# Corner sums through a PSUM tile, and a share of the corner multiply on GpSimd, in a deformable-convolution stage

## The chip, the cores and the metric

The kernel runs on one core of a Trainium2 chip. The metric is device time in microseconds for one execution, in fp32 throughout. The names of the engines in the profile are PE (TensorE), DVE (VectorE), ACT (ScalarE), POOL (GpSimd) and SP (the queue of SyncE, which only issues transfers). PEld is TensorE's loading of weights.

## The reference

The whole computation is a two-layer block on x of shape 2 x 128 x 64 x 64: a deformable convolution with four branches, a mixture of experts over tokens, a selective scan, and a second mixture of experts. The change lies in the first of these. For each output position and each tap of a branch, a learned offset gives a fractional position, and the input is sampled there bilinearly from four corners:

```
wy = (py - y0)[:, None]
wx = (px - x0)[:, None]
v00 = gather(y0, x0);      v01 = gather(y0, x0 + 1)
v10 = gather(y0 + 1, x0);  v11 = gather(y0 + 1, x0 + 1)
return v00 * (1 - wy) * (1 - wx) + v01 * (1 - wy) * wx + v10 * wy * (1 - wx) + v11 * wy * wx
...
sampled = bilinear_sample(x, py, px) * mask[:, None]
return jnp.einsum('bckhw,ock->bohw', sampled, reg_w.reshape(O, C, k * k))
```

The kernels of the four branches are 1x1, 1x1, 3x3 and 7x7, so that there are 1 + 1 + 9 + 49 = 60 taps (NTAP) for each position. C is 128, and each branch has 256 output channels.

## The kernel before

Positions are handled in groups of 512: four tiles (GT = 4) of 128 positions, one position to a partition. Each of the two images has 8 groups, so that there are 2 x 8 x 60 = 960 steps, called taps below. For every image a table in device memory holds, for each position, the 4 x 128 values of its four corners side by side, so that one row of 2 KB serves one sample.

The method `sample` runs the 60 taps of one group. For a tap it uses a buffer `v` of shape 128 x 4 x 512 (four tiles, and in each the four corners of 128 channels); there are six such buffers. `gather` (line 705) fills it with four indirect transfers, one for each tile, that are issued by GpSimd with row numbers from the tile `idx`. Then, on VectorE:

- line 746 multiplies all 2048 elements of a partition with the corner weights `pw`, broadcast over the 128 channels. `pw` is a copy in PSUM of the weights `w4`, made on line 738 for 30 taps at a time;
- line 748 adds corners 2 and 3 onto corners 0 and 1 (1024 elements);
- line 749 adds corner 1 onto corner 0 (512 elements).

All of these work in place in `v`. TensorE then transposes the four tiles into the PSUM tile `pst` (line 111), which is what frees `v`; ScalarE copies `pst` to `st` (line 753); and two taps later `product` multiplies `st` by the tap's weights `regw` on TensorE (line 773) and accumulates over the taps of a branch.

The order of work on TensorE, VectorE, ScalarE, GpSimd and SP is the order in which the program is written. The gathers of tap t+1 are written ahead of the arithmetic of tap t, and GpSimd, which has only gathers in this stage, runs ahead of VectorE as far as the six buffers go. At the end of each tap, pieces of other work are put in: `conv.step()`, the offset convolution (line 402 on TensorE) and the corner indices and weights of groups to come (lines 499 to 587, mostly VectorE), and `rest.step()`, the normalization of the second image, and, while the second image is sampled, the rest of the layers for the first one. After the sampling, in the last 2157 us, come the scan (lines 1420 to 1481) and the second mixture of experts.

PSUM has eight banks. While the first image is sampled `pw` takes one, `pst` two, `out` two, and the offset convolution with its companion two; while the second is sampled the last two go to the other work.

Of the kernel before, what the change touches and what calls it, by code (L numbers as in the profile page):

```python
# [10 lines left out]
F32 = mybir.dt.float32  # L11
I32 = mybir.dt.int32
AF = mybir.ActivationFunctionType
ALU = mybir.AluOpType
AX = mybir.AxisListType
PSUM = bass.MemoryType.PSUM
# [3 lines left out]
P = 128  # L20
B = 2
C = 128
# [3 lines left out]
GT = 4  # L26
# [9 lines left out]
NO = 3 * NTAP  # L36
TW = H + 3
E0 = 8
E1 = 64
HID = 512  # L40
DS = 16
# [143 lines left out]
class L0Conv:  # L185
# [416 lines left out]
    def run(self, build, after):  # L602

        env, tc, nc = self.env, self.env.tc, self.env.nc
        pools = lambda ctx: lambda name, bufs, **kw: ctx.enter_context(tc.tile_pool(name=name, bufs=bufs, **kw))
        with ExitStack() as ctx:
            pool = pools(ctx)
            self.rp, self.regw = pool("l0rw", 1), {}
            self.ip = pool("l0i", 2)
            self.vp = pool("l0v", 6)  # L610
            self.stp = pool("l0s", 2)
            self.pending, self.held = [], deque()
            first = ctx.enter_context(ExitStack())
            self.open_offsets(pools(first))
            for i in range(2):
                nc.vector.memset(self.padc[i], 0.0)
            psum = ctx.enter_context(ExitStack())
            right = lambda name: pools(psum)(name, 1, space=PSUM, side="right")
            self.p_f = deque([right("l0po")])
            cur = self.new_group(self.ip)  # L620
            with (
                tc.tile_pool(name="nrm", bufs=3) as sp,
                tc.tile_pool(name="nrmp", bufs=4, space=PSUM) as pp,
            ):
                xs = []
                for g in range(NG):
                    if g % GT == 0:
                        x = self.vp.tile([P, GT, 4 * C], F32, name="v")
                    xs.append(x[:, g % GT, :])
                    nc.sync.dma_start(out=xs[g], in_=env.d["x"][0, :, g * 512 : (g + 1) * 512])  # L630
                xn = self.vp.tile([P, GT, 4 * C], F32, name="v")
                self.load_weights()
                for _ in self.zero_table(0):
                    pass
                own = lambda g: xn[:, g % GT, :].rearrange("p (j c) -> p j c", c=C)
                norms = [self.norm_group(0, g, sp, pp, "nrm", x, own(g)) for g, x in enumerate(xs)]
                together(norms[:2], 2)

                stage = self.rows(0, 0)
                self.sum_weights()  # L640
                others = Side()
                others.add(mixed(norms[2:], 3))
                for _ in range(24):
                    others.step()
                offsets = self.offset_stream([(0, 0, cur)], stage)
                while others.todo:
                    next(offsets)
                    for _ in range(3):
                        others.step()
                self.load_chunk(0)  # L650
                for _ in self.norm_end(0):
                    pass
                for _ in offsets:
                    pass
            self.p_w = pool("l0pw", 1, space=PSUM)
            self.p_t = pool("l0pt", 2, space=PSUM)
            self.p_o = pool("l0py", 2, space=PSUM)
            self.pending = [(n, functools.partial(self.load_chunk, c)) for n, c in ((1, 1), (3, 2))]
            early = psum.enter_context(ExitStack())
            p_m = pools(early)("l0pm", 1, space=PSUM, side="right")  # L660

            def more():

                early.close()
                self.p_f.append(right("l0po2"))
                yield


            conv, rest = Side(), Side()
            self.late, self.made = deque(), [0, 0]  # L670
            rest.add(self.norm(1, p_m, "misc"), more(), build)
            ahead = {}

            def runs():
                for g in range(1, NG):
                    ahead[g] = self.new_group(self.ip)
                    yield 0, g, ahead[g]
                    yield 1, g - 1, None
                yield 1, NG - 1, None

            conv.add(self.offset_stream(runs()))
            for g in range(NG):
                self.sample(0, g, *cur, conv, rest, 2 if g else 3, lambda: ahead.get(g + 1))
                cur = ahead.get(g + 1)
            conv.drain()
            rest.drain()
            psum.close()
            first.close()
            side = ctx.enter_context(tc.tile_pool(name="l0ps", bufs=2, space=PSUM))
            rest.add(after(0, side))  # L690
            cur = self.load_group(1, 0)
            for g in range(NG):
                nxt = self.load_group(1, g + 1) if g + 1 < NG else None
                self.sample(1, g, *cur, conv, rest, 2, lambda: nxt)
                cur = nxt
            for f in self.late:
                f()
            for _, f in self.pending:
                f()
            self.pending = []  # L700
            rest.drain()
# [10 lines left out]
    def sample(self, b, g, idx, w4, conv, rest, pace, after):  # L712

        env, nc = self.env, self.env.nc
        pw, vs = None, {}
        new = lambda: self.vp.tile([P, GT, 4 * C], F32, name="v")

        def fetch(idx, t):
            if t in vs:
                v = vs.pop(t)  # L720
                self.gather(b, v, idx, t, range(2, GT))
            else:
                v = new()
                self.gather(b, v, idx, t, range(GT))
            return v

        if b == 0 and g == 0:
            for i in range(6):
                vs[i] = new()
                self.gather(b, vs[i], idx, i, range(0, 2))  # L730
        if not self.held:
            self.held.append(fetch(idx, 0))
        for br, (k, _) in enumerate(BRANCH):
            for t in range(FIRST[br], FIRST[br] + k * k):
                tw = t % HT
                if tw == 0:
                    pw = self.p_w.tile([P, GT, HT, 4], F32, name="pw")
                    nc.vector.tensor_copy(pw, w4[:, :, t : t + HT, :])
                if t + 1 < NTAP:
                    self.held.append(fetch(idx, t + 1))  # L740
                elif after():
                    self.held.append(fetch(after()[0], 0))
                v = self.held.popleft()
                v4 = v.rearrange("p j (q c) -> p j q c", q=4)
                w = pw[:, :, tw, :].unsqueeze(3).to_broadcast([P, GT, 4, C])
                nc.vector.tensor_tensor(v4, v4, w, ALU.mult)  # L746
                up = v4[:, :, 0:2, :]
                nc.vector.tensor_tensor(up, up, v4[:, :, 2:4, :], ALU.add)  # L748
                nc.vector.tensor_tensor(v4[:, :, 0, :], v4[:, :, 0, :], v4[:, :, 1, :], ALU.add)  # L749
                pt = self.p_t.tile([P, GT, P], F32, name="pst")  # L750
                transpose4(nc, env.ident, pt, [v4[:, j, 0, :] for j in range(GT)])
                st = self.stp.tile([P, 512], F32, name="st", bufs=3)
                nc.scalar.copy(st, pt.rearrange("p j t -> p (j t)"))  # L753
                self.late.append(functools.partial(self.product, b, g, br, t, st))
                if len(self.late) > 2:
                    self.late.popleft()()
                due = [f for n, f in self.pending if n == 0]
                self.pending = [(n - 1, f) for n, f in self.pending if n]
                for f in due:
                    f()  # L760
                conv.step()
                for _ in range(pace):
                    rest.step()
# [128 lines left out]
class L0Ffn:  # L892
# [3 lines left out]
    def __init__(self, env, dp, wp, gp):  # L896

        nc, d = env.nc, env.d
        self.env, self.dp, self.gp = env, dp, gp
        self.rw = wp.tile([P, E0], F32, name="rw")  # L900
        self.rb = wp.tile([P, E0], F32, name="rb")
        self.ew = wp.tile([P, E0 * C], F32, name="ew")
        self.eb = wp.tile([E0, C], F32, name="eb")
        self.tri = wp.tile([P, E0, E0], F32, name="tri")
        nc.sync.dma_start(out=self.rw, in_=d["router_w"])
# [993 lines left out]
```

## Time and profile before

| | |
|---|---|
| median of 3 runs | 7887.33 us (7886.47 to 7905.6) |
| the profiled execution's own time | 7901.31 us |
| its span, first to last instruction | 7898.7 us |
| sampling stage | to about 5742 us of the span |
| busy: PE, DVE, ACT, POOL | 68%, 77%, 25%, 64% of the span |
| mean granted clock of TensorE | 0.806 |

The profile has one line for each group of instructions: line, engine, operation, output and inputs, shapes, count; then the group's busy time in us and the mean of one in ns; then the idle time of the engine just ahead of these instructions, and what ended most of it. In a list of waits, a row says who waited for whom, the us in total, how many times and the longest. "issue" means that nothing the profile shows was waited for. In a timeline, a row has its start, its duration, and in brackets the idle time before it.

### The profile page before, as it was taken

To read this page: it belongs to the slowest core of one execution; us is meant where nothing else is said; L and a number is where in the kernel's file an instruction comes from. 1 tells how busy PE (TensorE), PEld (TensorE's weight loads), DVE (VectorE), ACT (ScalarE), POOL (GpSimd) and SP (SyncE) were. 2 spreads that over 40 slices of the span, in tenths; PEclk is the share of its full clock that TensorE was granted. 3 is DMA by queue.
4 is the path that set the end of the run, shared out by engine and by line. 5 is a ranking of instruction groups with operands and counts; after the bars stand their busy time and mean duration, and the time that the engine had idled before them with its cause. 6 is when DMAs were issued, how large, how long until landed. Compare 5 with 4: busy or idle time off the path is not lost. (4 is left out here: it accounts for less than half of the span.)

```text
span 7898.7 us, 67414 instructions
## 1 busy us (share of the span) xinstructions
PE 5390.6 (68%) x21313; PEld 3209.2 (41%) x21313; DVE 6077.1 (77%) x6780; ACT 1992.0 (25%) x3838; POOL 5031.9 (64%) x4589
## 2 busy tenths in 40 slices
PE   4667777667776757656666878865565679756668
PEld 3344444444444424324334555532233456412124
DVE  5878878888887887788898667787756665789992
ACT  1211111111111113211111222211163255455540
POOL 4777777777777777777777666676743334357640
PEclk8888788888788878878878778877886788877789
DMA  7887767777676778877777777777754344434444
GB/s 223 261 267 214 224 207 223 214 219 219 210 221 208 224 228 270 265 255 234 240 237 217 217 218 218 228 224 222 206 172 141 107 114 113 114 131 146 146 137 149
DMA packets 645198, 1596.67 MB, mean 202 GB/s; under 512 B 168020, under 2 KB 253180, under 8 KB 640876
## 3 DMA queue, kind: packets, MB, share of 16 engines
q0 software_dynamic: 307200, 1006.88, 42.5%
q1 hardware_dynamic: 306156, 537.52, 21.4%
q10 hardware_dynamic: 31488, 47.97, 1.7%
q8 instruction: 171, 2.80, 0.1%
q14 instruction: 183, 1.50, 0.1%
HBM read 1478.65 MB, written 115.83 MB: 202 GB/s over the span
## 5 line engine op out<-in xcount | busy, mean ns | idle before, releaser
L705 POOL DMA_INDIRECT v<-table,idx x3840 | 4070.0, 1060 | 1628.2 <-issue 1033.8
L746 DVE TENSOR_TENSOR v<-v,pw 128x2048 f32<-128x2048 f32 x960 | 2192.0, 2283 | 665.7 <-DMA v<-table,idx 466.9
L773 PE MATMUL out<-st,regw 128*128 128x512 f32 x3840 | 2270.7, 719 | 187.6 <-issue 118.6
L753 ACT COPY st<-pst 128x512 f32<-128x512 f32 x960 | 557.7, 585 | 4227.9 <-remote 1887.3
L111 PE MATMUL pst<-ident,v 128*128 128x128 f32 x3840 | 730.7, 318 | 1133.6 <-issue 962.4
L748 DVE TENSOR_TENSOR v<-v 128x1024 f32<-128x1024 f32 x960 | 1177.2, 1226 | 34.6 <-remote 1.6
L1420 POOL TENSOR_TENSOR db<-du,bcb 128x512 f32<-128x512 f32 x512 | 656.8, 1288 | 845.3 <-DVE da L1471 698.8
L773 PEld LDWEIGHTS out<-st,regw 128*128 128x128 f32 x3840 | 807.2, 233 | 864.6 <-issue 779.9
L111 PEld LDWEIGHTS pst<-ident,v 128*128 128x128 f32 x3840 | 522.4, 164 | 1512.3 <-issue 1284.6
L1443 PE MATMUL py<-sc,ident 128*128 128x512 f32 x1024 | 660.7, 752 | 230.7 <-DVE sc L1481 230.3
L1471 DVE TENSOR_TENSOR_SCAN da<-da,state,db 128x512 f32<-128x512 f32 x512 | 657.1, 1283 | 183.2 <-ACT da L1427 137.6
L749 DVE TENSOR_TENSOR v<-v 128x512 f32<-128x512 f32 x960 | 664.4, 692 | 33.0
L402 PE MATMUL po<-wa,win 128*128 128x147 f32 x2112 | 381.7, 303 | 118.1 <-issue 110.8
L402 PEld LDWEIGHTS po<-wa,win 128*128 128x128 f32 x2112 | 334.3, 201 | 228.7 <-issue 228.6
L1443 PEld LDWEIGHTS py<-sc,ident 128*128 128x128 f32 x1024 | 200.4, 229 | 529.9 <-DVE sc L1481 438.0
L1146 PEld LDWEIGHTS ps<-ipw,hs 128*120 128x120 f32 x2816 | 356.0, 207 | 121.7 <-ACT X L1108 56.4
L1146 PE MATMUL ps<-ipw,hs 128*120 128x64 f32 x2816 | 355.1, 290 | 55.2 <-ACT X L1108 40.5
L1481 DVE TENSOR_TENSOR sc<-da,bcb 128x512 f32<-128x512 f32 x512 | 354.2, 692 | 43.0 <-PE py L1443 0.5
L1427 ACT ACTIVATE da<-delta,w_A_log 128x512 f32<-128x512 f32 x512 | 354.0, 692 | 18.7 <-DVE delta L1383 2.8
L1154 PE MATMUL ps<-tm,X 120*88 120x48 f32 x2048 | 216.1, 280 | 52.1 <-ACT Y L1108 35.5
L1154 PEld LDWEIGHTS ps<-tm,X 120*88 120x88 f32 x2048 | 211.0, 187 | 98.7 <-ACT Y L1108 47.4
L402 PEld LDWEIGHTS po<-wb,win 128*128 128x128 f32 x960 | 164.2, 210 | 117.2 <-issue 117.1
(296 smaller groups left out, 4704.3 us busy)
## 6 DMA issues: line engine op xcount, KB each, us to landing
bcb<-bc SPq DMA_DIRECT2D x256, 512.0 KB
regw<-in_regw SPq DMA_DIRECT2D x192, 640.0 KB
v<-table,idx POOLq DMA_INDIRECT x3840
yd<-ys ACTq DMA_DIRECT2D x128, 256.0 KB
yc<-yd SPq DMA_DIRECT2D x32, 1024.0 KB
gb<-gd SPq DMA_DIRECT2D x16, 2048.0 KB
wt<-in_weight SPq DMA_DIRECT2D x32, 1024.0 KB
tm<-pos SPq DMA_DIRECT2D x16, 1440.0 KB
```

Of the source, the lines that this page charges most:

```text
L111: nc.tensor.transpose(ps[:, j, :], s, ident)
L402: m()
L705: self.env.nc.gpsimd.indirect_dma_start(out=v[:, j, :], out_offset=None, in_=self.table[b], in_offset=bass.IndirectOffsetOnAxis(ap=idx[:, ...
L746: nc.vector.tensor_tensor(v4, v4, w, ALU.mult)
L748: nc.vector.tensor_tensor(up, up, v4[:, :, 2:4, :], ALU.add)
L749: nc.vector.tensor_tensor(v4[:, :, 0, :], v4[:, :, 0, :], v4[:, :, 1, :], ALU.add)
L753: nc.scalar.copy(st, pt.rearrange("p j t -> p (j t)"))
L773: nc.tensor.matmul(self.out[half], self.regw[t // CH][:, t % CH, half * P : (half + 1) * P], st, start=first, stop=last,)
L1146: nc.tensor.matmul(ps[:, k, :], patch, own, start=True, stop=True)
L1420: nc.gpsimd.tensor_tensor(dbs[u], pieces[k]["du"][:, half, :], bcb[u // 2][:, 0, :], ALU.mult)
L1443: nc.tensor.matmul(py[k, half], by, what, start=first, stop=last)
L1471: nc.vector.tensor_tensor_scan(s, s, dbs.pop(u), state[:, half, n : n + 1], ALU.mult, ALU.add)
```

## The change

In every second tap (t odd, EVERY = 2) GpSimd multiplies the fourth corner with its weight, which it reads from `w4` in SBUF, and VectorE multiplies only the other three. In all taps the four corners are summed by three additions of 512 elements instead of one of 1024 and one of 512; the partial sum lies in a new PSUM tile `low`, of one bank, and the last addition writes corner 0 of `v`.

```
+EVERY = 2
...
+            self.p_r = pool("l0pr", 1, space=PSUM)
...
-                w = pw[:, :, tw, :].unsqueeze(3).to_broadcast([P, GT, 4, C])
-                nc.vector.tensor_tensor(v4, v4, w, ALU.mult)
-                up = v4[:, :, 0:2, :]
-                nc.vector.tensor_tensor(up, up, v4[:, :, 2:4, :], ALU.add)
-                nc.vector.tensor_tensor(v4[:, :, 0, :], v4[:, :, 0, :], v4[:, :, 1, :], ALU.add)
+                side = t % EVERY == EVERY - 1
+                if side:
+                    w = w4[:, :, t, 3:4].to_broadcast([P, GT, C])
+                    nc.gpsimd.tensor_tensor(v4[:, :, 3, :], v4[:, :, 3, :], w, ALU.mult)
+                end = 3 if side else 4
+                w = pw[:, :, tw, 0:end].unsqueeze(3).to_broadcast([P, GT, end, C])
+                nc.vector.tensor_tensor(v4[:, :, 0:end, :], v4[:, :, 0:end, :], w, ALU.mult)
+                low = self.p_r.tile([P, GT, C], F32, name="low")
+                nc.vector.tensor_tensor(low, v4[:, :, 0, :], v4[:, :, 1, :], ALU.add)
+                nc.vector.tensor_tensor(low, low, v4[:, :, 2, :], ALU.add)
+                nc.vector.tensor_tensor(v4[:, :, 0, :], low, v4[:, :, 3, :], ALU.add)
```

## The prediction

> **What bounds the kernel now.** I read the page first, then busy time by stretch, the waits of GpSimd and VectorE, and two timelines of the same ten microseconds. The page gives the per-tap prices.
>
> ```profile
> L705 POOL DMA_INDIRECT v<-table,idx x3840 | 4070.0, 1060 | 1628.2 <-issue 1033.8
> L746 DVE TENSOR_TENSOR v<-v,pw 128x2048 f32<-128x2048 f32 x960 | 2192.0, 2283 | 665.7 <-DMA v<-table,idx 466.9
> L748 DVE TENSOR_TENSOR v<-v 128x1024 f32<-128x1024 f32 x960 | 1177.2, 1226 | 34.6 <-remote 1.6
> L1420 POOL TENSOR_TENSOR db<-du,bcb 128x512 f32<-128x512 f32 x512 | 656.8, 1288 | 845.3 <-DVE da L1471 698.8
> L749 DVE TENSOR_TENSOR v<-v 128x512 f32<-128x512 f32 x960 | 664.4, 692 | 33.0
> ```
>
> VectorE spends 2.283 + 1.226 + 0.692 = 4.20 us on each of 960 taps, GpSimd 4 x 1.060 = 4.24 us on its four gathers. Both look equally loaded. The stretches decide.
>
> ```profile
> core 0: us, PE busy (x) PEld busy (x) DVE busy (x) ACT busy (x) POOL busy (x), PEclk, DMA share, GB/s
> 128.00:4300.00 4172.00, 2848.11 (x10637) 1715.28 (x10638) 3467.23 (x3772) 730.41 (x1358) 3055.45 (x2873) 0.82 0.75 232
> 4300.00:5410.00 1110.00, 830.76 (x4121) 555.82 (x4120) 809.22 (x602) 227.77 (x487) 760.87 (x727) 0.80 0.76 220
> 5410.00:5742.00 332.00, 180.78 (x483) 83.34 (x481) 258.57 (x207) 39.19 (x69) 237.31 (x225) 0.78 0.70 212
> ```
>
> In the first stretch 2873 gathers are 718 taps of 5.81 us. GpSimd is busy 4.25 of these, VectorE 4.83. But a gather is followed by a pause:
>
> ```profile
> POOL v L705 <- issue: 1029.2, 3374, 0.6
> POOL v L705 <- remote: 248.1, 120, 4.8
> POOL v L705 <- PE pst L111: 123.6, 96, 5.6
> ```
>
> 3374 times the pause is 0.305 us and nothing ended it: it belongs to the gather. Four of them make GpSimd's own work 4.25 + 1.22 = 5.47 of 5.81 us, so it truly waits (for a buffer of v that the transposes still hold) only 0.335 us a tap. In the second stretch (182 taps of 6.11 us, TensorE busy 75%) it works 5.41 and waits 0.70; in the third (56 taps of 5.90) 5.44 and some 0.34, its idle last 7 us left out. So GpSimd's queue sets the pace nearly throughout, and VectorE, idle about 1 us a tap, waits for gathers (466.9 us). The timelines show this, and a second thing:
>
> ```profile
> 1843.27 1.92 POOL L705 DMA_INDIRECT v<-table,idx  x1 [0.30 <-PE po L402]
> 1845.49 0.95 POOL L705 DMA_INDIRECT v<-table,idx  x1 [0.30 <-issue]
> 1846.75 0.95 POOL L705 DMA_INDIRECT v<-table,idx  x1 [0.30 <-issue]
> 1848.00 0.95 POOL L705 DMA_INDIRECT v<-table,idx  x1 [0.30 <-issue]
> ```
> ```profile
> 1843.15 1.23 DVE L748 TENSOR_TENSOR v<-v 128x1024 f32<-128x1024 f32 x1
> 1844.41 0.69 DVE L749 TENSOR_TENSOR v<-v 128x512 f32<-128x512 f32 x1
> 1845.90 2.29 DVE L746 TENSOR_TENSOR v<-v,pw 128x2048 f32<-128x2048 f32 x1 [0.80 <-DMA v<-table,idx]
> 1851.82 2.29 DVE L746 TENSOR_TENSOR v<-v,pw 128x2048 f32<-128x2048 f32 x1 [1.65 <-DMA v<-table,idx]
> ```
>
> These four gathers end at 1848.95, and VectorE starts on them 2.9 us later. And the gather that starts while line 748 runs takes 1.92 instead of 0.95 us, as if it could not read its indices until line 748 ended at 1844.38. Gathers beside the multiply, whose second operand lies in PSUM, take 0.95. So an addition with both inputs in SBUF holds a gather back; over the kernel that is 4070.0 - 3840 x 0.946 = 437 us, 0.91 per pair of taps.
>
> **The change, per pair of taps (an even and an odd one).**
>
> *VectorE.* The even tap costs 2.283 + 3 x 0.692 = 4.36. One element costs (2.283 - 1.226)/1024 = 1.03 ns, so in the odd tap the multiply loses 0.53 and the tap costs 3.83. I price additions through PSUM at 0.692: line 1481, which reads a PSUM tile and one in SBUF, takes 691 to 694 ns for 512 elements, and line 1471 works in place in PSUM. The mean is 4.10 instead of 4.20, 0.1 us a tap off an engine that already waits: nothing by itself.
>
> *GpSimd, added.* One 512-element multiply: 1.267 us (the median of line 1420; 1.252 to 1.747 over lines 1420 and 1330 beside other work, the broadcast weight being the untested part). Around it: it waits for four gathers' semaphores. Such a record takes 43 ns with about as much behind it, so two cost 0.17; bounds are -0.04 (line 1325's multiplies overlap by that) and 0.47 (a gather's pause as well). I take 0.17, the price seen on this queue.
>
> *The new waits.* The multiply of tap t stands behind the gathers of t+1 in GpSimd's queue, which take 5.0 us, and the data of t are there 2.9 us after their issue, so normally it finds them. Behind it are queued the gathers of t+2 and t+3. When a transfer is late these now wait too: between 0 and 0.49 (all 466.9 us that VectorE waits for DMA, over 960 taps); I take 0.12, near the bottom, as 2.1 us of slack cover the usual case. VectorE's last addition of an odd tap waits for GpSimd: the tap's data are usable at 2.9, its own work reaches that addition at 2.9 + 1.75 + 1.38 = 6.0, and GpSimd is done at 5.0 + 0.17 + 1.27 = 6.4. It waits 0.4 us, and behind it stand the transposes, the offset arithmetic and the next multiply, whose data come only at 7.9. The 1 us of idle time covers this; without that cover it costs 0.2 us a tap.
>
> *The port.* Only the first addition of a tap still has two SBUF inputs: 0.69 us to stall a gather in, instead of 1.23 + 0.69. A read met at random is held back by half the window and met in proportion to it, so the loss goes with the square. With only line 748 counted, 0.456 per tap becomes 0.456 x 0.692²/1.226² = 0.145; with a plain spacing of 1.25 us it is 0.692²/2.5 = 0.19. I take 0.17: 0.34 per pair, a relief of 0.57. Bounds: nothing left (0.91), or one full stall in every tap (1.38, a loss of 0.47). That addition may also meet the new multiply. In lines 1330 and 1333 such a meeting stretched both (1.267 to 1.747 on GpSimd, 0.740 to 1.755 on VectorE). By the clock above they touch for about 0.2 us, so I take 0.10, bounds 0 and 0.48.
>
> Here the Trainium skill says otherwise twice, on the page "SBUF — State Buffer", section "Who interferes with whom". It infers that a two-input addition takes only the shared read interface and so does not hold up descriptor generation; the 1.92 us gather contradicts it, and by the rule the relief would be 0 and the forecast about 250 us later. It also says that the second comer is blocked until the first has finished; the two stretched rows look like sharing, and by the rule the addition would wait out a whole multiply, on an engine that has the time.
>
> *Sum.* 1.267 + 0.17 + 0.12 + 0.10 - 0.57 = 1.09 per pair, 0.545 per tap. Against it stand GpSimd's present waits, 0.335, 0.70 and 0.34 a tap in the three stretches. They are bursts while TensorE holds buffers, so not all vanish: I leave 0.05. First stretch: 718 x (0.545 - 0.335 + 0.05) = 187. Second: the waits exceed the addition; I put 0.05 x 182 = 9. Third: 56 x 0.255 = 14. Together 210 us: the profiled execution of 7901.3 (span 7898.7) becomes 8111, and the median, 14 us lower at 7887.3, becomes 8097. After 5742 us nothing changes; the one new bank of PSUM is free in both phases (six banks and two make eight).
>
> **Rivals.**
>
> *Faster: the freed port pays for the multiply.* If no gather met the remaining addition (relief 0.91) and neither late data nor sharing cost anything, the pair costs 1.267 + 0.17 - 0.91 = 0.53, 0.265 a tap. It decides once relief passes 0.77 (1.267 + 0.17 - 2 x 0.335). Then 0.07 x 718 = 50 us are gained: 7837. For it: the stalls are large and visible. Against it: the additions still come 5 to 6 us after the gathers they depend on, where the next gathers are being issued.
>
> *Faster: VectorE is the pace after all*, and GpSimd's share costs nothing: 0.1 x 960 = 100 us, 7787. The 1 us that VectorE idles per tap speaks against it.
>
> *Slower by far: the multiply meets the addition each time.* GpSimd's multiply takes 1.747 and late data cost 0.2: 1.747 + 0.17 + 0.2 - 0.57 = 1.55, 0.77 per tap: 718 x 0.485 + 182 x 0.15 + 56 x 0.48 = 400 us, 8290. It decides where the additions lie wholly inside the multiply, which a shift of 0.7 us in the clock above brings about.
>
> *No change:* the waits absorb the addition wholly, 0.33 us a tap; this needs half of the priced cost to be wrong.
>
> **How the numbers follow.** About 0.3% (24 us) can be told from no change. The forecast, 8097, has a chance of 0.70, its own range 7990 to 8230; the freed port 0.08, VectorE's pace 0.03, no change 0.04, the meeting case 0.15. Faster is thus 0.11, same 0.04, slower 0.85. The range runs from 7880, leaving out the two faster rivals, to 8290, the meeting case, with its worse half outside.
>
> **What would show it.** Right: sampling ends near 5950 instead of 5742; GpSimd busy some 6.0 of a longer tap's 6.1 us, pauses included, its waits other than "issue" under a third of 380 us; mean gather under 1.03 us; new multiply about 1.3 us x480; VectorE's share of the stretch lower. Wrong: a mean gather unchanged (no relief), additions through PSUM far from 0.69, a multiply over 1.5, or taps no longer than 5.8 us.

## The result, and the profile after

The kernel after the change takes 7923.51 us (median of 15 runs, 7903.04 to 7936.1), the kernel before, run beside it, 7892.69 us (15 runs). The ratio is 1.0040, with a 95% interval of 1.0029 to 1.0050: slower by 31 us. The forecast was 8097, slower by 210 us. The direction is the forecast one and the time lies in the outer range given (7880 to 8290), but below the 7990 to 8230 of the forecast proper, and the size is about a seventh of it. Times of runs are medians; one execution of `hand_before`, at 10823 us, is left out as disturbed.

The profiled execution took 7931.86 us (span 7929.4), against 7901.31 before. From the first gather to the last transposes it is 5668.6 us instead of 5636.5; what follows takes 2151 instead of 2155 us. So all of the difference lies in the sampling stage. The page of the kernel after gives the new prices per tap:

```profile
L707 POOL DMA_INDIRECT v<-table,idx x3840 | 3797.2, 989 | 1313.4 <-issue 960.9
L753 DVE TENSOR_TENSOR v<-v,pw 128x2048 f32<-128x2048 f32 x960 | 1934.9, 2016 | 527.6 <-DMA v<-table,idx 393.8
L755 DVE TENSOR_TENSOR low<-v 128x512 f32<-128x512 f32 x960 | 898.4, 936 | 33.1
...
L757 DVE TENSOR_TENSOR v<-low,v 128x512 f32<-128x512 f32 x960 | 663.8, 691 | 97.2 <-POOL v L750 30.0
L756 DVE TENSOR_TENSOR low<-low,v 128x512 f32<-128x512 f32 x960 | 671.2, 699 | 33.0
...
L750 POOL TENSOR_TENSOR v<-v,w 128x512 f32<-128x512 f32 x480 | 511.0, 1065 | 115.7 <-DMA v<-table,idx 82.7
```

Line 707 is the gather (705 before), 750 the multiply on GpSimd, 753 VectorE's multiply, 755 to 757 the three additions. The gather fell from 1.060 to 0.989 us. The multiply takes 1.065 us, where 1.267 was forecast. The additions with one operand in PSUM take 0.691 and 0.699, but the first, with both in SBUF, has a mean of 0.936. Its median is 0.700: some of them are stretched. A tap's own instructions therefore cost VectorE 2.016 + 0.936 + 0.699 + 0.691 = 4.34 us in the mean, where they cost 4.20 before and 4.10 was forecast. Everything that VectorE does in the stage makes 4.92 us per tap (4.73 before), so the change gave VectorE more to do, not less. Busy time by stretch shows the same (columns: stretch, its length, then busy time of PE, PEld, DVE, ACT and POOL, granted clock, DMA share, GB/s):

```profile
128.00:4300.00 4172.00, 2840.95 (x10561) 1704.96 (x10561) 3584.74 (x4478) 732.12 (x1353) 3216.84 (x3222) 0.83 0.74 231
4300.00:5410.00 1110.00, 826.11 (x4148) 554.15 (x4146) 827.72 (x770) 224.30 (x480) 792.34 (x801) 0.81 0.75 216
5410.00:5742.00 332.00, 197.57 (x485) 88.49 (x484) 277.64 (x268) 42.92 (x75) 260.96 (x262) 0.77 0.72 220
```

In the first stretch VectorE is busy 3585 us (3467 before), GpSimd 3217 (3055), TensorE 2841 (2848). The waits of GpSimd in the sampling stage tell most (who waited, for whom, us in total, times, longest):

```profile
POOL v L707 <- issue: 956.9, 3298, 0.6
POOL v L707 <- remote: 80.1, 73, 5.4
POOL v L750 <- DMA v<-table,idx: 79.9, 25, 12.8
POOL v L707 <- DMA v<-table,idx: 78.0, 221, 2.0
POOL v L707 <- PE pst L112: 63.1, 77, 4.6
```

Before, "remote" was 248.1 and the wait for the transposes (line 111 then, 112 now) 123.6. Both are waits for a buffer of v that is still held, and both fell to a third or a half. New is the multiply's wait for late transfers, seldom (25 times) but up to 12.8 us long. The timeline of GpSimd shows what surrounds a multiply:

```profile
1845.01 0.95 POOL L707 DMA_INDIRECT v<-table,idx  x1 [0.30 <-issue]
1845.97 1.06 POOL L750 TENSOR_TENSOR v<-v,w 128x512 f32<-128x512 f32 x1
1847.19 1.26 POOL L707 DMA_INDIRECT v<-table,idx  x1 [0.16 <-issue]
...
1857.24 1.06 POOL L750 TENSOR_TENSOR v<-v,w 128x512 f32<-128x512 f32 x1
```

The multiply starts as the gather ends (0.017 us after it in the mean) and the next gather follows 0.158 us behind it. The pause of 0.305 us between gathers is not paid ahead of a multiply. VectorE at the same time:

```profile
1846.40 1.20 DVE L755 TENSOR_TENSOR low<-v 128x512 f32<-128x512 f32 x1
...
1851.36 0.70 DVE L755 TENSOR_TENSOR low<-v 128x512 f32<-128x512 f32 x1
...
1856.80 2.07 DVE L755 TENSOR_TENSOR low<-v 128x512 f32<-128x512 f32 x1
1858.91 0.70 DVE L756 TENSOR_TENSOR low<-low,v 128x512 f32<-128x512 f32 x1
```

The addition at 1856.80 was under way when the multiply of 1857.24 began, and took 2.07 instead of 0.70 us. The multiply took its usual 1.06. Where the two meet it is the addition that pays. The whole trace says the same. 724 of the 960 first additions meet no multiply and take 0.70 us, none over 0.78. 162 were under way when a multiply began and take 1.93 in the mean, 74 began during a multiply and take 1.04. The multiplies that they met take 1.06 in the mean.

**The account of GpSimd.** GpSimd's queue can be added up over the sampling stage: 3840 gathers at 0.946 us (3633 us in every kernel), what they were held back beyond that (stalls), the pauses of 0.305 us, the multiply, the gaps around it, and waits. Of the waits for buffers after the change, 86 us lie between two gathers and 55 between a multiply and the gather behind it (47 of these end with a step of the semaphore of TensorE's transposes). In us:

| | before | after |
|---|---|---|
| gather stalls | 437 | 165 |
| pauses | 3839 x 0.305 = 1171 | 3360 x 0.305 = 1025 |
| multiplies | - | 480 x 1.065 = 511 |
| gaps around them | - | 479 x (0.017 + 0.158) = 84 |
| waits before gathers, nearly all for buffers | 387 | 86 + 55 |
| waits before the multiply, mostly for late transfers | - | 105 |
| sum, with 3633 of gathers | 5628 | 5664 |
| stage by the trace | 5636 | 5669 |

Own work and the new wait add 511 + 84 + 105 - 146 (pauses) - 272 (stalls) = 282 us. The waits for buffers fell from 387 to 141 and gave back 246. That leaves 36, and the stage grew by 32.

### The profile page after: what moved, and what is told of

The parts are those of the page before. It is cut to its first block, busy times and chain, and to the rows that moved or that the text cites. A ratio compares the mean times of both kernels' runs of the same rounds, so it can differ in the third digit from the quotient of the medians.

```text
span 7929.4 us, 70291 instructions
## 1 busy us (share of the span) xinstructions
PE 5416.3 (68%) x21313; PEld 3214.5 (41%) x21313; DVE 6258.8 (79%) x7740; ACT 1997.5 (25%) x3838; POOL 5271.5 (66%) x5069
## 5 line engine op out<-in xcount | busy, mean ns | idle before, releaser
L707 POOL DMA_INDIRECT v<-table,idx x3840 | 3797.2, 989 | 1313.4 <-issue 960.9
L781 PE MATMUL out<-st,regw 128*128 128x512 f32 x3840 | 2294.1, 728 | 149.5 <-ACT ys L795 70.1
L753 DVE TENSOR_TENSOR v<-v,pw 128x2048 f32<-128x2048 f32 x960 | 1934.9, 2016 | 527.6 <-DMA v<-table,idx 393.8
L755 DVE TENSOR_TENSOR low<-v 128x512 f32<-128x512 f32 x960 | 898.4, 936 | 33.1
L757 DVE TENSOR_TENSOR v<-low,v 128x512 f32<-128x512 f32 x960 | 663.8, 691 | 97.2 <-POOL v L750 30.0
L756 DVE TENSOR_TENSOR low<-low,v 128x512 f32<-128x512 f32 x960 | 671.2, 699 | 33.0
L750 POOL TENSOR_TENSOR v<-v,w 128x512 f32<-128x512 f32 x480 | 511.0, 1065 | 115.7 <-DMA v<-table,idx 82.7
```

The source lines that it names most:

```text
L707: self.env.nc.gpsimd.indirect_dma_start(out=v[:, j, :], out_offset=None, in_=self.table[b], in_offset=bass.IndirectOffsetOnAxis(ap=idx[:, ...
L753: nc.vector.tensor_tensor(v4[:, :, 0:end, :], v4[:, :, 0:end, :], w, ALU.mult)
L755: nc.vector.tensor_tensor(low, v4[:, :, 0, :], v4[:, :, 1, :], ALU.add)
L756: nc.vector.tensor_tensor(low, low, v4[:, :, 2, :], ALU.add)
L757: nc.vector.tensor_tensor(v4[:, :, 0, :], low, v4[:, :, 3, :], ALU.add)
L781: nc.tensor.matmul(self.out[half], self.regw[t // CH][:, t % CH, half * P : (half + 1) * P], st, start=first, stop=last,)
```

## The experiments

The theory after the result: **GpSimd's queue** sets the pace of the sampling stage, with 387 us of waits as its reserve, and the price of the change is what the queue gets in addition, less that reserve. Rivals: **VectorE** is the pace (it has the highest busy share); **TensorE** holds the buffers and is a second limit close under the first. Each group below ran on one chip, with the kernel before beside it.

### One part at a time (chip 12; before 7891.43 us)

`sums_only` leaves the sums through PSUM and takes the multiply off GpSimd:

```
-EVERY = 2
+EVERY = 100
```

> Three additions through PSUM in all taps, GpSimd only gathers. Queue theory (GpSimd's queue sets the pace, and the multiply was cheaper than forecast: 1.065 us, of which 0.13 lie in the pause after a gather): the gathers' stalls fall from 437 to about 165 us as in the changed kernel, nothing is added to GpSimd, so it is faster than before by 100 to 250 us. VectorE theory (VectorE's time sets the pace): each tap has 0.16 us more of VectorE, so it is slower than before by 40 to 150 us. The first addition should take 0.70 us in all taps, as there is no multiply to meet.

`gpsimd_only` has the multiply on GpSimd and the two additions of before, without the PSUM tile:

```
+                up = v4[:, :, 0:2, :]
+                nc.vector.tensor_tensor(up, up, v4[:, :, 2:4, :], ALU.add)
+                nc.vector.tensor_tensor(v4[:, :, 0, :], v4[:, :, 0, :], v4[:, :, 1, :], ALU.add)
-                low = ...
```

> GpSimd multiplies the fourth corner in odd taps, the sums are the two SBUF additions of before. Queue theory: the multiply and its surroundings cost 0.93 us per pair, late data 0.2, and the stalls of gathers stay at 0.9 per pair, so 0.56 us per tap are added against waits of 0.335: slower than before by 150 to 250 us. VectorE theory: VectorE has 0.53 us less per pair and 0.5 more where line 748 meets the multiply, so within 50 us of before.

`pool_fill` is the kernel before with five small fills on GpSimd in every odd tap, `dve_fill` the kernel before with one reduction more on VectorE in every odd tap:

```
+                if t % 2:
+                    for _ in range(5):
+                        nc.gpsimd.memset(self.spare, 0.0)
```
```
+                if t % 2:
+                    nc.vector.tensor_reduce(self.spare[:, 0:1], pw.rearrange("p j t q -> p (j t q)"), AX.X, ALU.add)
```

> The kernel before, with five small fills (32 elements, no input) of a spare tile on GpSimd in every odd tap, about 1.1 us per pair, which read nothing and wait for nothing; VectorE's instructions are unchanged. Queue theory: about 0.5 us a tap more against waits of 0.335: slower by 80 to 200 us. VectorE theory: within 30 us of before.

> The kernel before, with one more VectorE instruction in every odd tap, a sum over the 480 elements of the weights in PSUM, about 0.65 us per pair; GpSimd's instructions are unchanged, and no port is shared. Queue theory: VectorE idles 1 us a tap, so within 40 us of before. VectorE theory: slower by 150 to 310 us.

| | us | ratio to before | gather stalls | waits of GpSimd | stage |
|---|---|---|---|---|---|
| sums_only | 7906.58 | 1.0024 (1.0011 to 1.0036) | 100 | 728 | 5640 |
| gpsimd_only | 8278.81 | 1.0493 (1.0468 to 1.0519) | 662 | 96 | 6016 |
| pool_fill | 8097.49 | 1.0268 (1.0247 to 1.0289) | 430 | 30 | 5835 |
| dve_fill | 7902.67 | 1.0020 (1.0007 to 1.0032) | 498 | 326 | 5636 |

In `pool_fill` the fills cost 1.17 us per pair of taps, their gaps included and the pause they replace taken off: 560 us on GpSimd. Groups and waits of it:

```profile
L748 POOL MEMSET spare<- 128x32 f32 x2400 | 308.0, 128 | 110.8
```
```profile
POOL v L706 <- PE pst L111: 37.9, 97, 1.9
```

The time rose by 206 us, and the waits fell from 387 to 30. 560 - 357 = 203: the reserve is spent first and the rest is paid in full. In `dve_fill` VectorE is busy 262 us longer than in the kernel before (6339 against 6077 us), and that costs 0.2%, 11 us. So GpSimd's queue paces once its waits are gone, and VectorE doesn't.

`gpsimd_only` shows what the sums through PSUM are worth beside the multiply. A group of it, and a wait of VectorE:

```profile
L706 POOL DMA_INDIRECT v<-table,idx x3840 | 4294.2, 1118 | 1180.3 <-issue 909.6 <-DMA table<-zero 71.3 <-DMA v<-table,idx 65.2
```
```profile
DVE v L754 <- POOL v L749: 410.6, 250, 3.0
```

The mean gather is 1.118 us, the stalls 662 (379 of them in gathers right behind a multiply), and 8 us of waits before gathers are left. The expectation, 150 to 250 us slower, was missed: it had the stalls unchanged at 0.9 us per pair, and they rose by 225 us. Also, VectorE now waits 411 us for GpSimd's multiply, since line 754 adds the fourth corner at once. Without the sums through PSUM the multiply makes the kernel 387 us slower, with them 31.

`sums_only` relieves the gathers most (stalls 437 to 100) and yet gains nothing here: 15 us slower, where one theory had at least 100 us faster and the other at least 40 slower. All that the queue was spared turned into waits:

```profile
POOL v L707 <- remote: 455.2, 166, 5.8
POOL v L707 <- PE pst L112: 252.7, 146, 11.6
```

These are the waits for buffers. Something other than GpSimd and VectorE holds the stage at about 5640 us, and the change of this case ends just above that: a second limit, which the next group was to find on TensorE.

### Prices, and TensorE's share (chip 1; before 7592.4 us)

`dense_weight` gives the multiply of the kernel after a dense operand, a tile of zeros, instead of the broadcast weight, so the fourth corner of odd taps counts as zero. `no_two_sbuf` multiplies corner 0 into PSUM, so that no addition has both inputs in SBUF. `before_half` and `sums_half` leave out one of the two matmuls of `product` in all but the first and last tap of a branch, in the kernel before and in `sums_only`.

```
-                    w = w4[:, :, t, 3:4].to_broadcast([P, GT, C])
+                    w = env.zero.rearrange("p (j c) -> p j c", j=GT)
```
```
+                nc.vector.tensor_tensor(v4[:, :, 1:end, :], v4[:, :, 1:end, :], w, ALU.mult)
...
+                nc.vector.tensor_tensor(low, v4[:, :, 0, :], w, ALU.mult)
+                nc.vector.tensor_tensor(low, low, v4[:, :, 1, :], ALU.add)
```
```
-        for half in range(2):
+        for half in range(2 if first or last else 1):
```

> The changed kernel, but GpSimd's multiply takes a dense tile of 512 elements (all zero, in place of the fourth corner's weight) instead of a weight broadcast over 128 channels. If the broadcast is what makes the multiply 1.065 us instead of the 1.267 of line 1420, it takes about 1.27 us here, and the time rises by up to 0.2 x 480 = 97 us over the changed kernel, of which GpSimd's remaining waits may take some. If the form of the operand does not matter, it stays at 1.06 and so does the time.

> The changed kernel with corner 0 multiplied straight into the PSUM tile, so that no addition has two inputs in SBUF: one more VectorE instruction per tap (about 0.16 us), no stretched first addition (it was 0.936 on average), no stalled gather (it was 165 us). Queue theory: GpSimd needs 165 us less, which the changed kernel could use for the 31 us that it is behind, so it equals the kernel before within 25 us. VectorE theory: VectorE's busy time falls only by some 0.08 us a tap, so at most 30 us faster than the changed kernel and more likely no different.

> The kernel before with one of the two products of line 773 left out for all taps of a branch but its first and last (half of the output channels of the third and fourth branch miss those taps): TensorE has 0.72 us less in 54 of 60 taps. Two-limits theory (GpSimd's queue with 5.47 us a tap, and TensorE's queue, which holds the buffers, with some 5.8): the time falls until GpSimd's own work is left, by 200 to 380 us. One-limit theory (GpSimd's queue or the transfers alone set the pace): within 60 us of before.

> As before_half, with the three additions through PSUM and no multiply on GpSimd. Two-limits theory: GpSimd's own work is 337 us less than in before_half, as its gathers are not stalled, so the relief of the port shows now: 100 to 300 us faster than before_half, VectorE (4.9 us a tap with little idle time) being the next limit. One-limit theory, with the transfers as the limit: no different from before_half.

| | us | ratio to before | gather stalls | waits of GpSimd | stage |
|---|---|---|---|---|---|
| dense_weight | 7928.59 | 1.0443 (1.0418 to 1.0468) | 181 | 111 | 5656 |
| no_two_sbuf | 7696.56 | 1.0140 (1.0118 to 1.0162) | 40 | 132 | 5429 |
| before_half | 7578.22 | 0.9984 (0.9971 to 0.9997) | 471 | 34 | 5317 |
| sums_half | 7315.02 | 0.9633 (0.9611 to 0.9656) | 84 | 155 | 5050 |

The first thing to see is the kernel before itself: 7592 us on this chip, where it took 7891 on the other. The expectations were written for the other chip. What they priced in us of the queue can be compared, what they said of the total can't without that.

The price of the multiply is told apart in one group:

```profile
L750 POOL TENSOR_TENSOR v<-v,zero 128x512 f32<-128x512 f32 x480 | 616.3, 1284 | 109.9 <-DMA v<-table,idx 96.5 <-DVE v L753 2.5 <-DVE low L756 2.1
```

With a dense operand it takes 1.284 us, as line 1420 did (median 1.267, mean 1.288). With the broadcast weight it is 1.061 to 1.065. The untested part of the forecast price, the broadcast weight, made 0.2 us.

In `no_two_sbuf` the gather is at 0.956 us, nearly undisturbed:

```profile
L707 POOL DMA_INDIRECT v<-table,idx x3840 | 3672.6, 956 | 1186.9 <-issue 869.7 <-DMA v<-table,idx 133.2 <-DMA table<-zero 69.7
```

The stalls go with the additions that have two inputs in SBUF: 430 to 498 us with two of them in a tap (1536 elements) and no multiply on GpSimd, 84 to 181 with one of 512, 40 with none. Its expectation, equal to before within 25 us, was missed by 104 us on a chip where the queue has little reserve to spend.

`before_half` was expected to gain 200 to 380 us and gained 14. TensorE was not the limit on this chip; GpSimd waits 34 us in it, and its queue sets the pace. Whether TensorE is the second limit on the other chip this run could not tell. `sums_half` gains 277 us, but so does `sums_again` below, which keeps TensorE's work whole.

### The same kernels on a third chip (chip 14; before 7586.85 us)

`before_again`, `after_again` and `sums_again` are the kernel before, the kernel after and `sums_only`, unchanged. `pe_fill` repeats two of the four transposes of a tap in the kernel before:

```
+                transpose4(nc, env.ident, pt, [v4[:, j, 0, :] for j in range(2)])
```

> The kernel before, unchanged, to have its profile on the chip of the runs beside it. In the first profile TensorE has 27 spells of some 10 us between 600 and 2800 us, 275 us together, in which it starts a matmul only every 0.7 to 1.4 us though nothing is waited for; in the profiles from the chip where the kernel before takes 7592 us there is none. Spell theory: the time is about 7590 us without spells and about 7890 with them, and GpSimd's waits are under 100 us without them and near 390 with them. Rival (the chips differ in something else, as the latency of transfers): no such link.

> The changed kernel, unchanged, on the same chip as the others of this group. Spell theory: where the kernel before has no spells, GpSimd's queue is its only limit, and the added 176 us of GpSimd's own work and some 100 of late data appear in full: slower by 150 to 300 us. Where it has spells, the waits that they make take it up: within 60 us. Rival: the same 31 us on every chip.

> Three additions through PSUM in all taps and no multiply on GpSimd, as in the earlier run. Spell theory: without spells the freed port shows, faster than before by 100 to 300 us; with them, within 30 us as in the earlier run. Rival: within 30 us on every chip.

> The kernel before with two of the four transposes of each tap issued twice (the same result in the same place), about 0.6 us of TensorE per tap. Spell theory, without spells: TensorE has room (4.0 busy of some 5.5 us), so within 60 us of before, unless the denser work itself brings the spells; with spells: TensorE's queue is a limit, slower by 50 to 300 us. Rival (GpSimd's queue or the transfers alone): within 60 us everywhere.

| | us | ratio to before | gather stalls | waits of GpSimd | stage |
|---|---|---|---|---|---|
| before_again | 7593.44 | (one run) | 477 | 48 | 5337 |
| after_again | 7797.92 | 1.0269 (1.0248 to 1.0291) | 174 | 111 | 5542 |
| sums_again | 7320.80 | 0.9648 (0.9630 to 0.9666) | 88 | 158 | 5058 |
| pe_fill | 7588.00 | 1.0004 (0.9989 to 1.0019) | 470 | 43 | 5325 |

The change itself costs 2.7% here, 211 us, and the sums alone are 3.5% faster. The waits of GpSimd in `before_again` show why:

```profile
POOL v L705 <- issue: 982.5, 3216, 2.9
POOL v L705 <- DMA v<-table,idx: 108.6, 266, 4.5
POOL v L705 <- PE pst L111: 47.5, 106, 5.3
```

The "issue" row and most of the second are the pauses. Waits for buffers come to 48 us in all, where they were 387. There is no reserve, so GpSimd's own work goes straight into the time: in `after_again` 509 + 84 - 146 - 303 = 144 us more of it, and 63 more of waits, 207 together, against 205 measured for the stage. Nearly all waits of `after_again` lie before the multiply:

```profile
POOL v L750 <- DMA v<-table,idx: 106.0, 53, 9.2
```

That is 0.22 us per pair. In `sums_again` stalls fall by 389 us and waits rise by 110; the stage is 279 us shorter:

```profile
L707 POOL DMA_INDIRECT v<-table,idx x3840 | 3720.4, 969 | 1398.9 <-issue 923.5
```

VectorE is busy 4.87 of its 5.27 us per tap, and would be next. `pe_fill` adds 1920 transposes at no cost; by the pages TensorE is busy 130 us longer (5356 against 5225), 0.14 us a tap, and not the 0.6 that the expectation had. It shows that the kernel has this much room on TensorE, and no more than that.

### The chips on which the kernel before takes 7890 us

In the profiles of chips 12 and 13, and in the first one, TensorE has stretches of about 10 us in which it starts a matmul only every 0.7 to 1.4 us though the profile shows nothing that it waits for. They are called spells below. One of them, in the timeline of the kernel before:

```profile
2016.01 0.29 PE L402 MATMUL po<-wa,win 128*128 128x147 f32 x1 [0.78 <-issue]
...
2018.84 0.58 PE L402 MATMUL po<-wb,win 128*128 128x147 f32 x1 [1.14 <-issue]
2020.21 0.40 PE L402 MATMUL po<-wb,win 128*128 128x147 f32 x1 [0.79 <-issue]
```

On the page, the idle time ahead of this line's matmuls tells the two kinds of chip apart. First the kernel before, then `before_again`:

```profile
L402 PE MATMUL po<-wa,win 128*128 128x147 f32 x2112 | 381.7, 303 | 118.1 <-issue 110.8
```
```profile
L402 PE MATMUL po<-wa,win 128*128 128x147 f32 x2112 | 341.9, 294 | 0.0
```

A count of such spells in the sampling stage (five or more weight loads in a row, each starting over 0.48 us after the one before and waiting for no semaphore). The number depends on such a rule, from 11 to 38 for the kernel before under nearby ones; the zeros don't:

| kernel | spells |
|---|---|
| before / after (first profiles) | 27 / 16 |
| sums_only / dve_fill / half_again (chip 12) | 23 / 21 / 16 |
| gpsimd_only / pool_fill (chip 12) | none |
| all eight on chips 1 and 14 | none |

The theory was that the spells are what holds the buffers, and so the reserve. The kernels `spell_before`, `spell_after` and `spell_sums` put 27 spells in by hand, in the kernel before, the kernel after and `sums_only`, by repeating the transposes of 27 taps 17 times (TensorE is then busy for as long, but starts its matmuls fast); `hand_before` and `hand_after` are the first two of them once more. `half_again` is `before_half` on chip 12.

```
+                n = g * NTAP + t
+                for _ in range(17 if b == 0 and 80 <= n < 460 and n % 14 == 3 else 1):
                     transpose4(nc, env.ident, pt, [v4[:, j, 0, :] for j in range(GT)])
```

> The kernel before, with spells made by hand: in 27 taps of the first image the four transposes are issued 17 times over (the same result in the same place), some 9 us of TensorE each. Spell theory: on a chip where the kernel before takes 7590 us this brings back a good part of the 300 us that separate it from 7890: slower by 60 to 300 us, and GpSimd's waits rise from 48 to some 150 to 400 us. Rival (spells are a mark of that chip and not the cause): within 40 us.

> The changed kernel with the same spells made by hand. Spell theory: the changed kernel loses much less by them than the kernel before, since GpSimd's longer work lies in the waits: it comes within 130 us of spell_before, where the two stand 211 us apart without spells. Rival: they stay about 210 us apart.

> Three additions through PSUM, no multiply on GpSimd, with the same spells made by hand. Spell theory: it loses more by them than spell_before, so that the 266 us that it gains without spells shrink, to under 180 us below spell_before. Rival: it stays some 266 us below spell_before.

> The kernel before with 27 spells made by hand, again, as the run before fell on a chip with spells of its own. If this chip has none (the kernel before at 7590 us). Spell theory: slower than before by 60 to 300 us, GpSimd's waits 100 to 400 us instead of 48. Rival: within 40 us. If the chip has its own: about 75 us slower than before, as there.

> The changed kernel with the same spells made by hand. On a chip without spells of its own, spell theory: within 130 us of hand_before (the two are 211 us apart without spells). Rival: about 210 us apart. On a chip with its own: within 60 us, as there.

> The kernel before with one of the two products of line 773 left out for all taps of a branch but its first and last, again. On a chip with spells of its own, spell theory: TensorE has 0.72 us less to do in most taps and makes up for the spells in between, or has none, so 150 to 320 us faster than before. Rival (the chip's GpSimd or transfers are slower): within 60 us. On a chip without: within 30 us, as in the earlier run.

| | us | ratio to before | waits of GpSimd | spells by the count above |
|---|---|---|---|---|
| spell_before (chip 13, before 7896.65) | 7972.6 | 1.0091 (1.0059 to 1.0123) | 438 | 17 |
| spell_after | 8001.78 | 1.0143 (1.0118 to 1.0169) | 295 | 11 |
| spell_sums | 8005.9 | 1.0133 (1.0100 to 1.0165) | 822 | 24 |
| hand_before (chip 12, before 7890.18) | 7956.3 | 1.0086 (1.0057 to 1.0116) | 389 | 20 |
| hand_after | 7988.01 | 1.0118 (1.0094 to 1.0142) | 312 | 10 |
| half_again | 7885.74 | 0.9992 (0.9975 to 1.0008) | 343 | 16 |

Both chips turned out to be of the kind with spells, so these kernels had the chip's spells and mine. Stretches by hand cost the kernel before 76 and 66 us. The change stays 29 and 32 us above it, as it does without them, and `spell_sums` has 822 us of waits and no gain. On top of the chip's own spells this tells nothing of whether such stretches make the reserve; on a chip without spells, where it could be told, it wasn't tried. The experiment is inconclusive.

`half_again` was expected to be 150 to 320 us faster if the spells or TensorE's load were the limit; it took the same time as before. It takes a matmul of `product` out of nearly every tap (TensorE is busy 4818 us instead of 5391), and spells and waits for buffers stayed:

```profile
POOL v L705 <- remote: 192.4, 96, 4.6
```

So TensorE's amount of work is not what limits these chips either, and taking work off TensorE doesn't end the spells. Its expectation named a rival that would give the same time: gathers or transfers that are slower on this chip. The traces speak against it. The median gather is 0.946 us in the kernel before and 0.947 in `before_again`, and the packets of the gathers' queue took 42.5% of 16 engines' span of 7899 us and 44.3% of 7591, which is the same time within 0.2%. The granted clock of TensorE differs too (0.806 in the kernel before, 0.840 in `before_again`), but the time doesn't follow it: `half_again` takes 7886 us at 0.745 and `before_half` 7578 at 0.770.

What the spells leave out is visible on another engine. "Remote" in these lists is a wait that ended with a step of a semaphore near which the profile has no instruction ending. Here are ScalarE's copies of `pst`, which wait for TensorE, in the kernel before and in `before_again`, and then a place in the kernel before where there is no spell:

```profile
L753 ACT COPY st<-pst 128x512 f32<-128x512 f32 x960 | 557.7, 585 | 4227.9 <-remote 1887.3
```
```profile
L753 ACT COPY st<-pst 128x512 f32<-128x512 f32 x960 | 562.5, 586 | 3886.0 <-PE pst L111 3869.6
```
```profile
2857.19 3.62 PE L773 MATMUL out<-st,regw 128*128 128x512 f32 x4
...
2866.96 1.07 ACT L753 COPY st<-pst 128x512 f32<-128x512 f32 x2 [10.73 <-remote]
2867.14 0.94 POOL L705 DMA_INDIRECT v<-table,idx  x1 [4.77 <-remote]
...
2867.60 1.11 PE L111 MATMUL pst<-ident,v 128*128 128x128 f32 x4 [6.79 <-ACT st L753]
```

TensorE's matmuls on record end at 2860.8, and ScalarE and GpSimd, both waiting for TensorE, go on together 6 us later, when its semaphore makes eleven steps within 1.1 us, after none since 2855.57. In `before_again` a step follows the end of its matmul by 0.014 us in the median, and 5 of 5320 come over 2 us late or are missing; in the kernel before 1686 of 5320 do, in the kernels with spells 26 to 38%, in `gpsimd_only` and `pool_fill` 14%, and in the eight runs on chips 1 and 14 at most 0.3%.

GpSimd's "remote" waits are waits for this semaphore (248.1 us in the kernel before, none in `before_again`). They go on where the count has no spell: 98.0 of the 248.1 us lie after 2800 us, and its last spell ends at 2770. So what sets these chips apart is that others learn late of TensorE's work, in the whole stage, and a spell is at most one form of it. That TensorE's signals come late there is shown. Why, and whether TensorE itself ran late or only its signal, is open, as is the part that the profile's own recording has in it: of all semaphores it has 48622 steps in the kernel before and 104034 in `before_again`.

## Why the prediction was right or wrong

**What bounds the kernel, and that its waits absorb: right.** The forecast took GpSimd's queue as the pace and its waits as the reserve. It added 1.09 us per pair (523 us) and let the waits take up 313 of them. Measured, 282 us were added, and the waits for buffers took up 387 - 141 = 246. `pool_fill` and `gpsimd_only` show the same from the other side: there the waits ran out, and the rest was paid.

**The port: the number right to the hundredth, in part by luck.** Relief 0.57 us per pair was forecast; (437 - 165)/480 = 0.57 was measured, and 0.63 on chip 14. The estimate by squares, 0.34 us of stalls left per pair, met 165/480 = 0.34, but from two errors. Without the multiply (`sums_only`) the additions leave 100 us, 0.21 per pair, less than the squares gave. The multiply brings the rest, as 91 of the 165 us lie in the gathers right behind one; the forecast had no such term. The rule of the Trainium skill that the prediction weighed (page "SBUF — State Buffer", section "Who interferes with whom"), by which a two-input addition wouldn't hold descriptor generation, would have made the relief 0. The stalls of these runs, 437 to 40 us as the two-input additions in SBUF go, decide against it.

**The terms that were mis-sized, per pair.** This is the step of the sum that failed:

| term | forecast | measured | over 480 pairs |
|---|---|---|---|
| the multiply | 1.267 | 1.065 | -97 |
| its surroundings | 0.17 | 0.017 + 0.158 - 0.305 = -0.13 | -144 |
| late data | 0.12 | 105/480 = 0.22 | +48 |
| sharing | 0.10 | 0 | -48 |
| port relief | -0.57 | -0.57 | 0 |
| sum | 1.09 | 0.585 | -241 |

The measured terms make 282 us; less the 246 that the waits took, 36, against 32 in the stage. Put into the forecast's own sum they make 718 x (0.293 - 0.335 + 0.05) + 9 = 15 us, so it is these terms that failed, more than the rule for the waits. The largest miss is the surroundings. The forecast priced them by semaphore records on this queue; in the trace a multiply takes the place of a pause between two gathers, and so pays for part of itself. The bound below nothing given there (-0.04) was too near. Next comes the price of the multiply: its row was that of a dense operand, and `dense_weight` shows that the broadcast weight makes the 0.2 us. The error in late data went the other way. The prediction's slack of 2.1 us covers the usual case, but 25 waits of up to 12.8 us, 80 of the 105, carry the term, and a mean lag of 2.9 us from a timeline doesn't show them.

**Sharing: wrong engine.** The prediction let a meeting stretch both, by lines 1330 and 1333. Here GpSimd's multiply keeps its 1.06 us and VectorE's first addition takes up to 2.07. Without the stretching the tap would cost 4.11 us, as forecast; with it VectorE's gain of 0.1 us a tap became a loss of 0.14 (4.20 to 4.34). Its share of the stretch rose, where the prediction had named a lower share as a sign of being right. It cost little, as VectorE doesn't pace (`dve_fill`: 0.2%). The second rule weighed there, from the same page and section, has the order of issue decide who is blocked (that the other is blocked fully it says of VectorE's two-port modes). At 1846 us VectorE came second and lost; at 1856.80 it came first and lost as well, and so in the mean of 74 and 162 such meetings (1.04 and 1.93 us). The order of arrival didn't decide in this trace.

**The rivals.** "The freed port pays" had the relief at 0.91; it was 0.57, but the queue came near that rival through the cheaper multiply instead. "VectorE is the pace" fell with `dve_fill`. "The multiply meets the addition each time" had GpSimd at 1.747 us; no mean is near that (its sum also used 0.15 where its terms make 0.12, 5 us more; and line 1420, quoted as reaching 1.747 with line 1330, has one of 2.252). "No change" was given 0.04 as it needs half of the priced cost to be wrong. 241 of 523 us were, and the result lies 31 us from it.

**What the forecast didn't see.** 31 us is the price where the kernel before has 387 us of waits. On chip 14, where it has 48, the same change costs 211 us. The forecast of 210 is the same number by accident: there the terms were smaller and hardly any waits took them up.

**A better version.** The sums through PSUM without the multiply (`sums_only`, `sums_again`) are 3.5% faster than before on chip 14, where the kernel after is 2.7% slower, and beat both kernels there. On chip 12 they are within 0.3% of before (1.0024), so that half of the change is worth keeping and the multiply on GpSimd isn't.

## What to carry to other kernels

Add up the queue of the engine that paces as own work, pauses, stalls and true waits, and set a change against the waits first: they took up 246 of the 282 us added here, and 357 of 560 in `pool_fill`, where they ran out. A kernel with many waits hides both a loss and a gain. Price a moved operation by a row with the same operand form and the same neighbours in its queue: a broadcast operand and a pause that was no longer paid made 0.50 of the 1.44 us that were forecast for the multiply and its surroundings. A part that gains nothing alone on one chip may be the one that wins on another, so run parts and whole on the same chip.

## What the runs showed of the hardware

- An indirect gather is held up by VectorE additions with both inputs in SBUF (stalls of 437 us in 3840 gathers of the kernel before), and hardly by those with one operand in PSUM (40 us in `no_two_sbuf`).
- On GpSimd a multiply of 512 elements takes 1.061 to 1.065 us with a broadcast operand and 1.284 with a dense one.
- Where such a multiply and a VectorE addition with both inputs in SBUF overlap, the addition is stretched (0.70 to 1.93 us in the mean if it came first, 1.04 if it came second), and the multiply keeps 1.06.
- A gather is followed by 0.305 us of pause before another gather, by 0.017 us before a multiply, and the gather after a multiply comes 0.158 us behind it.
- The same kernel takes 7587 to 7592 us on chips 1 and 14 and 7890 to 7897 on chips 12 and 13. The difference lies in waits of GpSimd for buffers (48 against 387 us), and goes with late steps of TensorE's semaphore (over 2 us late or missing for 32% of its matmuls, against 0.1%). The cause is open.
